# The next image's first layernorm: both halves abreast, with its additions ahead of the convolution's last taps

## The chip, the cores and the metric

The kernel runs on one core of a Trainium2 chip. The metric is device time in microseconds (us); a version's time is the median of its runs. Five engines matter: TensorE (PE; matmuls, weight loads are shown as PEld), VectorE (DVE), ScalarE (ACT), GpSimd (POOL; here it only issues DMAs that add into their destination, "folds") and SyncE (SP; plain DMAs). Each engine runs its own instructions in order and waits for semaphores that others raise.

## What is computed

Eight images of 384 channels and 32 x 32 positions go through a transformer block and then a ConvNeXt block, all in float32:

```python
# layer 0, per image: tokens xf of shape (1024, 384)
xn = layernorm(xf, g1, beta1)                    # "ln1", the first layernorm
q, k, v = xn @ w_qkv.T + b_qkv                   # 8 heads of 48
out = softmax(q @ k.T * SCALE) @ v
x1 = out @ w_proj.T + b_proj + xf
xn2 = layernorm(x1, g2, beta2)                   # "ln2", the second
h = gelu(xn2 @ w_fc1.T + b_fc1)                  # 384 -> 1536
x = x1 + h @ w_fc2.T + b_fc2
# layer 1, per image
y = depthwise_conv_7x7(x) + dw_b                 # 49 taps
y = layernorm(y, ln_w, ln_b)                     # "ln3", the third, over channels
y = gelu(y @ w1 + b1)
y = y * (gx / (mean(gx) + eps)) * gamma + beta + y   # gx: norm of each channel
x = x + y @ w2 + b2
```

## The kernel before

An image lies in SBUF as three tiles of 128 channels with 1024 positions each (`[P, CT, N]`); a "half" is 512 positions. Channels lie on partitions, so a layernorm over channels sums over partitions, with TensorE and a matrix of ones.

**One layernorm.** `layernorm` (from L486) makes a half in ten VectorE operations: two additions over the three channel tiles (L500, L503), three subtractions of the mean (L510), two additions of the three squares (L521, L524) and three scalings (L538). ScalarE makes the squares (L517) and the inverse root as a logarithm and an exponential (L534, L535). The sums over partitions are in `token_sums` (from L460). With `fold` it first lets GpSimd issue a DMA that adds one half of the partitions onto the other (L475), and then multiplies by 64 rows of ones instead of 128 (L481): half 0 uses partitions 0 to 63, half 1 uses 64 to 127. `abreast` runs the chains of both halves step by step together, `both` one after the other.

**The planner.** `Flow` writes the order of the instructions. Work beside the matmuls is a Python generator, a chain, that issues some instructions and yields a number of us of TensorE time after which it goes on. `flow.pe(us)` moves that clock by the planned length of a matmul (`U` = 0.857 us for a 128 x 512 one) and steps the chains that are due. `after(first, chain)` starts a chain when another has ended, `flow.finish` issues all that is left of one at once. So what stands ahead of what in an engine's queue is fixed when the program is built.

**One image.** For image b the order is: q and k, attention (with b + 1 loaded into `xn` in its middle), `mlp(b)`, then for image b - 1 `grn_up` (w1), the start of the convolution of b, values of b + 1 and `grn_down` (w2). `mlp` runs fc1 as 12 hidden tiles for half 0 and 12 for half 1 (`gelu_half`, L378: three matmuls of two passes each into a PSUM bank of the pool `ps_o`, four banks; a GELU by ScalarE, L457, empties it), while ln2 of half 1 runs beside them. Then `by_thirds` makes fc2 with 15 products of four matmuls each (L445) in place of 18, by sums and differences of the hidden tiles: pairs named e, f, g, h and d in the code, `hid` and `fc_e` in the profile. Most are made by VectorE in operations of 1024 columns (L953), g and the second h by folds (L965). Products of even number take a bank of `ps_o`, odd ones a tile of `ps_s` (two tiles of two banks). Results are added into `x` by VectorE (L950, L953) and copied into the padded image `pad` by ScalarE (L887).

**The convolution** of image b - 1 is 42 taps a channel tile on VectorE (L1098), spread over the stages before, and 7 that ScalarE multiplies and GpSimd's folds add (`help_convolution`, L1119, L1120; its scratch tiles have the tag `res`, four buffers). It must have ended before ln3 of image b - 1, and ln3 before `make_thirds` (L404, ten operations) and `grn_up` (L416).

**Where the two layernorms meet.** `conv_norm(b, ln)` is called in fc1 of image b, after hidden tile 3 of half 0, and starts two chains that wait for ln2's end: ln3 of image b - 1 (on `acc`, both halves abreast) and ln1 of image b + 1 (on `xn`). For b from 2 to 6, ln3's chain first issues the rest of the taps (`end_soon`), waits 16 us, and goes on with ln3's additions; ln1's chain waits 24 us and makes half 0 and then half 1 (`halves_of_next`). For b = 1, ln3 waits for the convolution's own end, and ln1 starts 1 us after ln2. Image 0 and image 7 go other ways.

Of the kernel before, what the change touches and what calls it, by code (L numbers as in the profile page):

```python
# [46 lines left out]
F32 = mybir.dt.float32  # L47
AF = mybir.ActivationFunctionType
ALU = mybir.AluOpType
AX = mybir.AxisListType  # L50

P = 128
B, C, H, W = 8, 384, 32, 32
N = H * W
CT = C // P
# [6 lines left out]
NH = N // 2  # L62
# [4 lines left out]
U = 0.857  # L67
# [108 lines left out]
def block_kernel(  # L176
# [15 lines left out]
    nc = tc.nc  # L192
# [5 lines left out]
    three = ctx.enter_context(tc.tile_pool(name="three", bufs=3))  # L198
# [3 lines left out]
    ps_s = ctx.enter_context(tc.tile_pool(name="ps_s", bufs=2, space=PSUM))  # L202
    ps_o = ctx.enter_context(tc.tile_pool(name="ps_o", bufs=4, space=PSUM))
    flow = Flow()
# [7 lines left out]
    def half(h):  # L212
        return slice(h * NH, (h + 1) * NH)
# [4 lines left out]
    def load_x(b, tag, parts=2, engine=nc.sync):  # L218
        xt = one.tile([P, CT, N], F32, tag=tag, bufs=2 if tag == "xn" else 1, name=f"{tag}_{b}")
        src = image_of(x, b).rearrange("(c p) n -> p c n", p=P)  # L220
        for i in range(parts):
            cols = slice(i * N // parts, (i + 1) * N // parts)
            engine.dma_start(out=xt[:, :, cols], in_=src[:, :, cols])
        return xt
# [4 lines left out]
    ones = const.tile([P, P], F32, name="ones")  # L229
    eps0 = const.tile([P, 1], F32, name="eps0")  # L230
# [19 lines left out]
    def col(name, i):  # L250
        at, width = VEC[name]
        assert i < width
        return vec[:, at + i : at + i + 1]
# [7 lines left out]
    def o_tile(name):  # L261
        return ps_o.tile([P, NH], F32, tag="o", name=name)
# [188 lines left out]
    def ln_table():  # L451
        if table[0] != "ln":
            nc.scalar.preload_act_table_set("natural_log_exp_and_others")
        table[0] = "ln"
# [5 lines left out]
    def token_sums(t, name, fold, wait):  # L460

        width = t.shape[-1]
        if fold is None:
            total = o_tile(name)[:, :width]
            nc.tensor.matmul(out=total, lhsT=ones, rhs=t, start=True, stop=True)  # L467
            flow.pe(U * width / NH)
            return [(total, slice(0, width))]
        rows = [slice(0, 64), slice(64, P)]  # L470
        parts = [(fold, slice(0, width))]
        if fold == "columns":
            parts = [(j, slice(j * width // 2, (j + 1) * width // 2)) for j in range(2)]
        for j, cols in parts:
            nc.gpsimd.dma_start(out=t[rows[j], cols], in_=t[rows[1 - j], cols], accum_op=ALU.add)  # L475
        yield wait
        totals = []
        for j, cols in parts:
            total = o_tile(f"{name}_{j}")[:, : cols.stop - cols.start]
            for i in rows:  # L480
                nc.tensor.matmul(out=total[i, :], lhsT=ones[rows[j], :64], rhs=t[rows[j], cols], start=True, stop=True)  # L481
            flow.pe(U * width / NH / 2)
            totals.append((total, cols))
        return totals

    def layernorm(src, dst, h, eps, g, name, switch, spare=None, spaced=False, slow=1.0, fold=None, wait=3.4, gentle=False):  # L486

        cols = h if isinstance(h, slice) else half(h)
        if isinstance(h, slice):
            h = h.start
        width = cols.stop - cols.start
        if spare:
            a, *squares = (t[:, :width] for t in spare())
            rstd = a
        else:
            a = one.tile([P, NH], F32, tag="ln_a", name=f"{name}_a{h}")[:, :width]
        nc.vector.tensor_tensor(a, src[:, 0, cols], src[:, 1, cols], ALU.add)  # L500
        if gentle:
            yield 1.2
        nc.vector.tensor_tensor(a, a, src[:, 2, cols], ALU.add)  # L503
        yield 2.6 * slow
        totals = yield from token_sums(a, f"{name}_sum{h}", fold, wait)
        yield 0.8
        for ct in range(CT):
            for total, part in totals:
                to, of = dst[:, ct, cols][:, part], src[:, ct, cols][:, part]
                nc.vector.scalar_tensor_tensor(to, total, -1.0 / C, of, ALU.mult, ALU.add)  # L510
            if gentle:
                yield 1.2
        yield 0.8 * slow
        if not spare:
            squares = [three.tile([P, NH], F32, tag="ln_sq", name=f"{name}_sq{h}_{ct}")[:, :width] for ct in range(CT)]
        for ct in range(CT):
            nc.scalar.activation(squares[ct], dst[:, ct, cols], AF.Square)  # L517
            if spaced:
                yield 1.7
        yield 0.8 if spaced else 1.8 * slow  # L520
        nc.vector.tensor_tensor(squares[0], squares[0], squares[1], ALU.add)  # L521
        if gentle:
            yield 1.2
        nc.vector.tensor_tensor(squares[0], squares[0], squares[2], ALU.add)  # L524
        yield 1.8 * slow
        totals = yield from token_sums(squares[0], f"{name}_var{h}", fold, wait)
        yield 0.8

        if not spare:
            rstd = one.tile([P, NH], F32, tag="ln_rstd", name=f"{name}_rstd{h}")[:, :width]  # L530
        if switch:
            ln_table()
        for var, part in totals:
            nc.scalar.activation(rstd[:, part], var, AF.Ln, bias=eps, scale=1.0 / C)  # L534
        nc.scalar.activation(rstd, rstd, AF.Exp, scale=-0.5)  # L535
        yield (2.6 if switch else 1.2) * slow
        for ct in range(CT):
            nc.vector.scalar_tensor_tensor(dst[:, ct, cols], dst[:, ct, cols], col(g, ct), rstd, ALU.mult, ALU.mult)  # L538
            if gentle and ct < CT - 1:
                yield 1.2  # L540
# [767 lines left out]
    def sequence(*chains):  # L1308
        for chain in chains:
            yield from chain  # L1310

    def after(first, chain, us=0):
        if us:
            yield us
        while first is not None and first.gi_frame is not None:
            yield 1.0
        yield from chain
# [293 lines left out]
    def main():  # L1611
# [5 lines left out]
        xn = load_x(0, "xn", 4)  # L1617
# [31 lines left out]
        t = three.tile([P, 2, NH], F32, tag="p", name="wqk_beta1").rearrange("p a n -> p (a n)")[:, : 2 * C]  # L1649
        for k in range(CT):  # L1650
            weighted(t, wqk_in(large[0])[:, k, :, :].rearrange("p m o -> p (m o)"), "beta1", k)
        ps = o_tile("bqk")
# [5 lines left out]
        state = {"help": None, "xn": xn, "conv": None, "acc": None, "norm1": None, "norm3": None}  # L1658
# [8 lines left out]
        def conv_norm(b, ln):  # L1667

            if b == 0:
                xn = state["xn"]  # L1670
                norm = abreast(xn, xn, eps0, "g1", "ln1_1", True, gentle=True)
                state["norm1"] = flow.spawn(after(ln, norm))
            else:
                acc = state["acc"]
                how = dict(wait=5.0) if b < B - 1 else dict(wait=3.4, factor=2.4)
                norm = abreast(acc, acc, eps1, "lnw", f"ln3_{b - 1}", True, **how)
                if 1 < b < B - 1:
                    state["norm3"] = flow.spawn(after(ln, sequence(end_soon(b), norm)))
                    state["norm1"] = flow.spawn(after(ln, halves_of_next(b, 24.0)))
                else:  # L1680
                    state["norm3"] = flow.spawn(after(ln, after(state["help"], after(state["conv"], norm))))
                if b == 1:
                    state["norm1"] = flow.spawn(after(ln, halves_of_next(b, 1.0)))

        def next_image(b):
            if b + 1 < B:
# [14 lines left out]

        def end_soon(b):
            end_convolution(b)
            yield 16.0

        def res_places(name):
            return [three.tile([P, NH], F32, tag="res", bufs=4, name=f"{name}_{i}") for i in range(4)]

        def halves_of_next(b, us):
            yield us  # L1710
            xn = state["xn"]
            for h in range(2):
                name = f"ln1_{b + 1}"
                places = lambda: res_places(f"{name}_{h}")
                yield from layernorm(xn, xn, h, eps0, "g1", name, True, spare=places, fold=h, wait=5.0, gentle=True)

        def before_fc2(b):

# [35 lines left out]
        for b in range(B):  # L1754
# [8 lines left out]
            ln2, rest, xn = attention(b, xt, *q_and_k, (folding, aside) if b == 0 else (), next_image)  # L1763
# [21 lines left out]
            if b < B - 1:  # L1785
# [4 lines left out]
                scale = flow.spawn(grn_scale(b - 1, gx, weights, b - 1, y))  # L1790
# [6 lines left out]
            else:  # L1797
# [4 lines left out]
                scale = flow.spawn(grn_scale(b - 1, gx, weights, b - 1))  # L1802
                flow.finish(state["norm_a"])
                sums = small.tile([P, CT, HT], F32, tag="gx_last", bufs=1, name="gx_last")
# [17 lines left out]
        scale = flow.spawn(grn_scale(B - 1, gx, weights, B - 1))  # L1822
# [143 lines left out]
```

## Time and profile before

| what | value |
|---|---|
| median of 3 runs | 3322.22 us (3320.67 to 3322.98) |
| the profiled execution, whole | 3318.74 us |
| its span, first to last instruction | 3316.9 us |
| granted TensorE clock, mean | 0.991 |
| L481, sums of 64 rows, ln1 (`ln_sum<-ln`) | 48 passes, median 640 ns |
| L1098, a tap on VectorE | 861, mean 1156 ns, 963.6 us busy |
| DMA into SBUF by GpSimd, `acc<-tap` | 294, 256 KB each, 3.6 us to landing |
| instructions | 38888 |

The span is one execution, taken by the hardware profiler. "Busy" counts overlapping instructions of an engine once. The profile names an instruction by engine, line and program names, with buffer numbers left out, so `ln<-ln` is any scratch tile of ln1. A matmul of float32 shows as two passes, so 'x4' there is two matmuls. A wait is put down to the semaphore that came last by the profile; where several came close together, it can have been another.

### The profile page before, as it was taken

What the parts mean: (1) busy time and instruction counts of PE and PEld (TensorE: products, weight loads), DVE (VectorE), ACT (ScalarE), POOL (GpSimd) and SP (SyncE); (2) the same over time, 40 slices, a digit from 0 to 9 for tenths busy, and PEclk for the clock granted to TensorE, in tenths of its full rate; (3) what the DMA queues carried; (4) which work ended last, traced back from release to release, by engine and by line L of the source; (5) the groups of instructions that cost most, each with busy time, mean ns of one, the idle gap of its engine ahead of it and who ended that gap; (6) DMA issues with size and microseconds to landing.
All of it is one profiled execution on the core that took longest, in us unless ns stands there. A gap on an engine that the chain in (4) does not pass through costs nothing. (4 is left out here: it accounts for less than half of the span.)

```text
span 3316.9 us, 38888 instructions
## 1 busy us (share of the span) xinstructions
PE 3260.0 (98%) x14216; PEld 1408.2 (42%) x14216; DVE 2431.7 (73%) x3318; ACT 1666.4 (50%) x2319; POOL 480.7 (14%) x567
## 2 busy tenths in 40 slices
PE   9999999999999999999999999999999999999999
PEld 5344434343344433444343443434434344444456
DVE  4644788787876878768787687866877778879850
ACT  3442763357644475354762647527474275723631
POOL 2121211112110121101211012110221102200000
PEclk9999999999999999999999999999999999999999
DMA  6635742547335573546635374353843538433231
GB/s 211 220 99 122 163 86 60 148 111 170 79 74 140 127 149 76 102 119 156 135 61 116 103 188 100 60 125 104 201 89 64 135 96 198 78 77 89 62 94 55
DMA packets 202707, 384.83 MB, mean 116 GB/s; under 512 B 41104, under 2 KB 47120, under 8 KB 202128
## 3 DMA queue, kind: packets, MB, share of 16 engines
q0 software_dynamic: 81472, 166.50, 26.8%
q1 hardware_dynamic: 120752, 215.09, 21.5%
q8 instruction: 114, 1.87, 0.2%
q10 hardware_dynamic: 288, 0.71, 0.1%
q14 instruction: 81, 0.66, 0.1%
HBM read 199.61 MB, written 38.14 MB: 72 GB/s over the span
## 5 line engine op out<-in xcount | busy, mean ns | idle before, releaser
L1098 DVE SCALAR_TENSOR_TENSOR acc<-pad,vec,acc 128x870 f32<-128x870 f32 (+8 forms) x861 | 963.6, 1156 | 6.6 <-DMA acc<-tap 1.7
L764 ACT ACTIVATE p<-s 128x1024 f32<-128x1024 f32 x512 | 524.6, 1025 | 275.3 <-PE s L755 267.3
L755 PE MATMUL s<-qk 48*64 48x512 f32 x4096 | 548.1, 593 | 0.2 <-ACT qk L601 0.2
L775 PE MATMUL o<-p,v 64*64 64x512 f32 x4096 | 545.6, 591 | 0.0
L378 PE MATMUL fc<-xn,fc 128*128 128x512 f32 x1152 | 505.0, 594 | 2.0 <-DVE acc L510 2.0
L1120 POOL DMA_DIRECT2D acc<-tap x294 | 253.6, 874 | 1337.6 <-ACT tap L1119 701.6
L378 PEld LDWEIGHTS fc<-xn,fc 128*128 128x128 f32 x1152 | 216.7, 190 | 286.0 <-issue 269.6
L445 PE MATMUL fc_p<-hid,fc 128*128 128x512 f32 x728 | 330.8, 611 | 0.0
L457 ACT ACTIVATE hid<-fc,bfc_f 128x512 f32<-128x512 f32 x192 | 131.1, 686 | 325.5 <-PE fc L378 325.4
L775 PEld LDWEIGHTS o<-p,v 64*64 64x64 f32 x4096 | 168.6, 133 | 275.8 <-issue 269.7
L755 PEld LDWEIGHTS s<-qk 48*64 48x64 f32 x4096 | 164.1, 133 | 276.4 <-issue 223.3
L445 PE MATMUL o_p<-y,w 128*128 128x512 f32 x624 | 270.9, 592 | 0.0
L445 PEld LDWEIGHTS fc_p<-hid,fc 128*128 128x128 f32 x728 | 141.5, 196 | 189.3 <-issue 185.4
L1119 ACT ACTIVATE tap<-pad,vec 128x512 f32<-128x512 f32 x294 | 215.9, 735 | 0.5 <-DMA acc<-tap 0.4
L445 PEld LDWEIGHTS o_p<-y,w 128*128 128x128 f32 x624 | 118.0, 190 | 148.7 <-issue 134.9
L1098 DVE SCALAR_TENSOR_TENSOR acc_last<-pad,vec,acc_last 128x377 f32<-128x377 f32 (+24 forms) x288 | 177.3, 690 | 0.6
L887 ACT COPY pad<-x 128x512 f32<-128x512 f32 x48 | 30.2, 634 | 285.6 <-DVE x L953 227.3
L716 DVE TENSOR_TENSOR attn<-o,attn 128x512 f32<-128x512 f32 x64 | 44.1, 689 | 124.5 <-ACT attn L714 124.5
L697 PE MATMUL proj<-attn,wproj_sb 128*128 128x512 f32 x288 | 127.7, 596 | 1.2 <-DVE attn L742 1.1
L675 PE MATMUL v<-wv_sb,xn 128*128 128x384 f32 x384 | 126.8, 487 | 0.0
L432 DVE TENSOR_TENSOR y<-h_n,y 128x512 f32<-128x512 f32 x72 | 49.8, 692 | 71.3 <-PE h_n L416 68.8
L675 PEld LDWEIGHTS v<-wv_sb,xn 128*128 128x128 f32 x384 | 72.5, 190 | 50.1 <-issue 3.3
(374 smaller groups left out, 4100.3 us busy)
## 6 DMA issues: line engine op xcount, KB each, us to landing
acc<-tap POOLq DMA_DIRECT2D x294, 256.0 KB, 3.6
fc<-s_fc SPq DMA_DIRECT2D x91, 256.0 KB, 4.3
w<-s_w SPq DMA_DIRECT2D x72, 320.0 KB, 3.0
hid<-hid POOLq DMA_DIRECT2D x42, 512.0 KB, 6.8
fc<-in_wfc SPq DMA_DIRECT2D x54, 384.0 KB, 4.0
w<-s_w SPq DMA_DIRECT2D x78, 256.0 KB, 2.7
y<-y POOLq DMA_DIRECT2D x36, 512.0 KB, 6.7
w_A<-in_w SPq DMA_DIRECT2D x36, 384.0 KB, 3.2
```

The lines of the kernel that those rows point to most:

```text
L378: nc.tensor.matmul(out=ps, lhsT=lhsT(k), rhs=rhs(k)[:, half(h)], start=(k == 0), stop=(k == nk - 1))
L432: nc.vector.tensor_tensor(c[dst], banks(name), c[other], ALU.add)
L445: nc.tensor.matmul(out=bank, lhsT=lhsT, rhs=rhs, start=k == 0, stop=k == len(pairs) - 1)
L457: nc.scalar.activation(dst, src, function, **kw)
L675: nc.tensor.matmul(out=ps[:, :C], lhsT=xn[:, k, t * P : (t + 1) * P], rhs=wv_sb[:, k, :], start=(k == 0), stop=(k == CT - 1),)
L697: nc.tensor.matmul(out=ps, lhsT=wproj_sb[:, m, ct * P : (ct + 1) * P], rhs=attn[:, m, :], start=(m == 0), stop=(m == CT - 1),)
L755: nc.tensor.matmul(out=s[64 * i : 64 * i + 64, j, :], lhsT=kT[64 * j : 64 * j + HD, m, k0 : k0 + 64], rhs=qT[64 * j : 64 * j + HD, m, half ...
L764: nc.scalar.activation(p, s, AF.Exp)
L775: nc.tensor.matmul(out=outs[i][64 * j : 64 * j + 64, :], lhsT=v[keys, t, at : at + 64], rhs=p[keys, j, :], start=(t == 0), stop=(t == KT - 1),
L1098: nc.vector.scalar_tensor_tensor(dst, window, tap, dst, ALU.mult, ALU.add)
L1119: nc.scalar.mul(t.rearrange("p (h w) -> p h w", w=W), window, tap)
L1120: nc.gpsimd.dma_start(out=acc[:, ct, half(h)], in_=t, accum_op=ALU.add)
```

## The change

`halves_of_next` is replaced by `norm_of_next`, which makes both halves of ln1 side by side:

- The four additions and the two folds of ln1 come as soon as ln2 has ended. Its chain is started before ln3's, so they stand ahead of the taps that `end_soon` issues.
- 22 us later (34 for b = 1) come the four sum matmuls, both halves one after the other, into tiles of `ps_s` instead of `ps_o`, then three subtractions a half, with squares of two channel tiles issued between them.
- The third square goes into the tile of the sums once the first addition of squares has read it, so that four `res` tiles serve both halves.
- After the folds of the squares it waits 8 us, then makes the variances, the inverse roots and six scalings, 1.2 us apart.
- For b = 1 the rest of the taps is also issued at ln2's end, with ln3's additions 28 us later.

```diff
@@ -1674,13 +1674,11 @@
                 acc = state["acc"]
                 how = dict(wait=5.0) if b < B - 1 else dict(wait=3.4, factor=2.4)
                 norm = abreast(acc, acc, eps1, "lnw", f"ln3_{b - 1}", True, **how)
-                if 1 < b < B - 1:
+                if b < B - 1:
+                    state["norm1"] = flow.spawn(after(ln, norm_of_next(b, 22.0 if b > 1 else 34.0)))
                     state["norm3"] = flow.spawn(after(ln, sequence(end_soon(b), norm)))
-                    state["norm1"] = flow.spawn(after(ln, halves_of_next(b, 24.0)))
                 else:
                     state["norm3"] = flow.spawn(after(ln, after(state["help"], after(state["conv"], norm))))
-                if b == 1:
-                    state["norm1"] = flow.spawn(after(ln, halves_of_next(b, 1.0)))
 
         def next_image(b):
             if b + 1 < B:
@@ -1701,18 +1699,63 @@
 
         def end_soon(b):
             end_convolution(b)
-            yield 16.0
-
-        def res_places(name):
-            return [three.tile([P, NH], F32, tag="res", bufs=4, name=f"{name}_{i}") for i in range(4)]
-
-        def halves_of_next(b, us):
+            yield 16.0 if b > 1 else 28.0
+
+        def norm_of_next(b, us):
+
+            xn, name = state["xn"], f"ln1_{b + 1}"
+            places = [three.tile([P, NH], F32, tag="res", bufs=4, name=f"{name}_{i}") for i in range(4)]
+            pairs = [(h, places[2 * h], places[2 * h + 1]) for h in range(2)]
+            rows = [slice(0, 64), slice(64, P)]
+
+            def fold(t, h):
+                nc.gpsimd.dma_start(out=t[rows[h], :], in_=t[rows[1 - h], :], accum_op=ALU.add)
+
+            def total(t, h, kind):
+                if kind == "sum":
+                    ps = ps_s.tile([P, N], F32, tag="s", name=f"{name}_sum{h}")[:, :NH]
+                else:
+                    ps = o_tile(f"{name}_var{h}")
+                for i in rows:
+                    nc.tensor.matmul(out=ps[i, :], lhsT=ones[rows[h], :64], rhs=t[rows[h], :], start=True, stop=True)
+                flow.pe(U / 2)
+                return ps
+
+            for h, a, _ in pairs:
+                nc.vector.tensor_tensor(a, xn[:, 0, half(h)], xn[:, 1, half(h)], ALU.add)
+            for h, a, _ in pairs:
+                nc.vector.tensor_tensor(a, a, xn[:, 2, half(h)], ALU.add)
+                fold(a, h)
             yield us
-            xn = state["xn"]
-            for h in range(2):
-                name = f"ln1_{b + 1}"
-                places = lambda: res_places(f"{name}_{h}")
-                yield from layernorm(xn, xn, h, eps0, "g1", name, True, spare=places, fold=h, wait=5.0, gentle=True)
+            sums = [total(a, h, "sum") for h, a, _ in pairs]
+            yield 0.8
+            for h, a, square in pairs:
+                for ct in range(CT):
+                    part = xn[:, ct, half(h)]
+                    nc.vector.scalar_tensor_tensor(part, sums[h], -1.0 / C, part, ALU.mult, ALU.add)
+                    if ct < 2:
+                        nc.scalar.activation((square, a)[ct], part, AF.Square)
+                yield 3.0
+            for h, a, square in pairs:
+                nc.vector.tensor_tensor(square, square, a, ALU.add)
+                nc.scalar.activation(a, xn[:, 2, half(h)], AF.Square)
+                yield 1.5
+            for h, a, square in pairs:
+                nc.vector.tensor_tensor(square, square, a, ALU.add)
+                fold(square, h)
+            yield 8.0
+            sums = [total(square, h, "var") for h, _, square in pairs]
+            yield 0.8
+            ln_table()
+            for h, a, _ in pairs:
+                nc.scalar.activation(a, sums[h], AF.Ln, bias=eps0, scale=1.0 / C)
+                nc.scalar.activation(a, a, AF.Exp, scale=-0.5)
+            yield 4.0
+            for h, a, _ in pairs:
+                for ct in range(CT):
+                    part = xn[:, ct, half(h)]
+                    nc.vector.scalar_tensor_tensor(part, part, col("g1", ct), a, ALU.mult, ALU.mult)
+                    yield 1.2
 
         def before_fc2(b):
```

## The prediction

> **What bounds the kernel now.** I read the page first, then the list of waits of TensorE, then the timeline of one image, then the granted clock after each stop.
>
> ```profile
> PE 3260.0 (98%) x14216; PEld 1408.2 (42%) x14216; DVE 2431.7 (73%) x3318; ACT 1666.4 (50%) x2319; POOL 480.7 (14%) x567
> ```
>
> TensorE is busy 3260.0 of 3316.9 us: only what shortens its work or its 57 us of idle time counts. (The chain of work that ended last reaches back only to 2946 us and shows the last image, which the change leaves alone.) The list of TensorE's waits over the span (total, times, longest, in us) puts half of the idle time on one place:
>
> ```profile
> PE ln_sum L481 <- DVE hid L953: 12.7, 3, 4.3
> PE ln_var L481 <- DMA ln<-ln: 8.9, 6, 3.5
> PE ln_sum L481 <- DMA ln<-ln: 7.9, 2, 4.0
> ```
>
> The tile `ln` is the scratch of the next image's first layernorm (ln1), so 12.7 + 8.9 + 7.9 = 29.5 us are waits of its sum matmuls. The timeline of image 2 (start, length, engine, line, operation, passes, idle time before it) shows where:
>
> ```profile
> 964.02 0.65 PE L481 MATMUL ln_sum<-ln_a,ones 64*64 64x512 f32 x2
> 965.04 6.28 PE L378 MATMUL fc<-xn,fc 128*128 128x512 f32 x14
> 965.14 3.68 DVE L510 SCALAR_TENSOR_TENSOR acc<-ln_sum,acc 128x512 f32<-128x512 f32 x6 [10.60 <-PE ln_sum L481]
> 971.25 1.08 PE L481 MATMUL ln_sum<-ln,ones 64*64 64x512 f32 x4
> 972.25 1.98 PE L378 MATMUL fc<-xn,fc 128*128 128x512 f32 x4
> ...
> 981.14 0.75 DVE L950 SCALAR_TENSOR_TENSOR x<-fc_p,vec,x 128x512 f32<-128x512 f32 x1 [6.62 <-PE fc_p L445]
> ...
> 1010.18 0.85 POOL L475 DMA_DIRECT2D ln<-ln  x1 [4.56 <-DVE ln L503]
> ...
> 1015.19 1.29 PE L481 MATMUL ln_sum<-ln,ones 64*64 64x512 f32 x4 [4.20 <-DVE hid L953]
> 1016.41 6.00 PE L445 MATMUL fc_p<-hid,fc 128*128 128x512 f32 x10
> ```
>
> Three things. The second half of ln1 is queued on VectorE among fc2's additions; its fold is issued only at 1010.18, and TensorE stands 4.20 us before the sum at 1015.19. (The releaser named is a VectorE addition that ended then. The fold that the sum needs takes 2.7 to 6.1 us to land there, so it comes down at the same moment; in two of the five images the fold itself is named.) VectorE meanwhile had 10.60 and 6.62 us idle, earlier. And the third layernorm (ln3), whose halves run abreast, needs 965.04 - 964.02 = 1.02 us of TensorE for both sums, ln1 972.25 - 971.25 = 1.00 us for one half. Last, 10 us windows from the restart after each long stop (length, TensorE busy, clock, DMA share and GB/s):
>
> ```profile
> 609.59:619.59 10.00, 10.00 (x17) 0.66 0.62 117
> 1015.19:1025.19 10.00, 10.00 (x21) 0.83 0.12 33
> 1418.02:1428.02 10.00, 10.00 (x21) 0.83 0.12 34
> 1819.54:1829.54 10.00, 10.00 (x19) 0.73 0.12 34
> 2221.69:2231.69 10.00, 10.00 (x18) 0.70 0.12 32
> 2624.25:2634.25 10.00, 10.00 (x18) 0.69 0.11 31
> ```
>
> The clock is below 1 after each: a "busy" TensorE is slow there.
>
> **What the Trainium skill says.** "TensorE: Matmul & The Clock Gate", Part 1 (The HAM clock gate): after an idle window of about 3.4 us TensorE falls to half clock until it has been busy for about as long. The trace agrees: idle of 3.46 to 4.28 us is followed by 0.66 to 0.83, idle of 1.08 us by none (a window from 1036.37 has 1.00). The same page, Part 3 (Packing small matmuls): matmuls on different row groups of the array run at the same time; the 1.02 against 1.00 us above is that. Its section "Architectural detail" calls ScalarE's and VectorE's queues strict FIFO; here a GELU (971.62) stands behind six squares. "DMA: Bandwidth & Descriptors", Anatomy of one DMA (SWDGE): about 2.0 us plus bytes by 436 GB/s, so an estimate of 2.3 us for a 131 KB fold. Here two folds that met little other traffic took 2.7 us, others up to 6.1.
>
> **The change part by part.** Image 2 (block b = 2) stands for b = 2 to 6, whose orders are alike; b = 1 is apart. Counts stay the same (20 VectorE operations, 10 ScalarE operations, 4 folds, 8 matmuls of 64 rows an image), SP's order too.
>
> *Gone: the idle time.* 3.46 us in b = 1, then 4.20 + 1.08, 4.28 + 1.07, 4.22 + 1.10, 3.87 + 1.08, 4.00 + 1.09: 29.5 us, if the new places of the sums have none.
>
> *Gone: the slow clock.* Ten us times one minus the clock: 3.4 + 1.7 + 1.7 + 2.7 + 3.0 + 3.1 = 15.6 us.
>
> *Gone: half of ln1's matmul time.* Sum and variance, one pair of 1.02 instead of two singles of 1.0: 2.0 us an image, 12.0 us. Together 57.1 us.
>
> *The additions ahead of the last taps.* Four additions at a pitch of 0.61 push the 13 taps back by 2.4 us: VectorE ends them at 952.9 instead of 950.4 and ln3's additions at 955.7 (953.2). ln3's folds then go out at about 954.4 and 956 and land, with the 5.6 and 6.2 us that the same two took, at 960 and 962. TensorE wants them at 964.2: covered by 2 us. In GpSimd's queue ln1's folds pass the first `fc2_e` fold, and nothing else waits there.
>
> *TensorE's new order* (0.43 us a pass). Hidden tile 6 of the second half starts at 956.3. After two of its matmuls come ln1's sums at 958.0; after two of tile 8 ln3's at 964.2; fc1 ends at 973.8; product 0 to 977.2; within product 1 ln1's variances at 978.9, after it ln3's at 981.7; product 2 at 982.7, 3 at 986.1, 4 at 989.6, 5 at 993.0.
>
> *The subtractions, squares and second additions.* ln1's six subtractions fill VectorE's idle time, 959.1 to 962.7. Before each ScalarE square stands one, so the GELU of tile 6 is at 961.0 instead of 958.98; its bank is wanted at 964.7. ln3's six: 965.3 to 968.9. Only then come ln1's additions (968.9, 969.5), so the third square of half 0 is at 969.6. Behind it on ScalarE stand six squares of ln3 (0.52 each), the third square of half 1 (973.3 to 973.9) and the GELUs of tiles 9 to 11, of which tile 9's is at 973.8 instead of 967.92. Their banks are wanted from 978.9, so no one waits. Half 1's last addition is over at 974.6, its fold lands 2.7 us after issue at 977.6, wanted at 978.9. ln3's four additions end at 977.6, the last fold lands at 980.6, wanted at 981.7. Both covers are only about 1.1 to 1.3 us.
>
> *The scalings: a new wait.* VectorE gets product 1 at 981.9, then two differences f (1.13 each), one scaling, two additions that wait for product 2 (986.3), a scaling, h0 (ends 989.4), ln3's six scalings (4.0), a scaling, h1 (ends 995.2), an addition for the thirds, x, a scaling, e0 (998.2), two more, e1 (1000.7). Before, one h and one e stood ahead of ln3's scalings: h1 ended at 988.8, e0 at 990.0 and e1 at 995.7. Product 5 wants h1 at 994.7 (0.5 late); product 6 wants e0 at 996.9 (1.3) and e1 at 1000.0 (0.75). New stalls: 2.55 us, too short for the clock to fall. The rest runs free: VectorE's next debts (f'' at 1017.7 for 1019.6, d at 1021.7 for 1026.5) are met, products 7 to 14 follow at 3.43 us. At the start of grn_up the copies for padding stand ahead of the first copy of `y`, some 0.2 us late, which the variance stop used to hide. Cost: 2.75 us an image, 13.8 us in five.
>
> *Block 1.* Its 21 taps are now emitted at once instead of spread, but end at about 559, and the sums stand after fc1's end (568.1), so these are covered. GpSimd's two g folds stand behind ln3's square folds, which end late. By the same rows: product 5 waits 0.9 for h1, ln3's variance 0.3, product 7 about 1.3 for its fold, products 11 and 12 0.8 and 1.6, and grn_up's fourth matmul 1.4 us more than the 1.88 it waits now for `y` behind late padding copies: 6.3. I take 5, since a later wait partly takes up an earlier one.
>
> *Sum.* 57.1 - 13.8 - 5 = 38.3 us. The profiled execution took 3318.7 us (span 3316.9 and 1.8 around it), so 3280.4; the median of the runs is 3.5 us above that execution, so 3322.2 - 38.3 = 3283.9 us.
>
> *Bounds.* The folds' landing has no row for its new traffic: with 2.3 us (the page's estimate) the stalls stay as above; with 6.1 (the longest here) each variance comes 2 to 3 us late, and ln3's scalings and h1, e0, e1 with it, 3 to 6 us an image. I take 2.7. VectorE's pitch is known, but a few operations in other places move h1 and e1 by 1.5 us either way, from no stall at all to 5 us an image. ScalarE's late GELUs cost 0 to 2.
>
> **The rivals.**
> *No new wait.* VectorE and the folds keep up everywhere: 57 us are won, 3265. For it: 17 us of idle VectorE in each image. Against: h1 and e0 stand behind six more scalings.
> *VectorE becomes the bound of fc2.* The differences come 5 to 6 us late in each image, the gain falls to about 57 - 30 - 7 = 20 us, 3302. For it: from 981 to 1002 VectorE has no idle time in my count. Against: ln1's whole second half has left it.
> *Slower: ScalarE's queue holds both layernorms.* The third square of ln1 stands ahead of ln3's squares and three GELUs, and itself behind ln3's subtractions. If ln3's folds land behind the sums, everything on ScalarE and the variances slip, and each stop of over 3.4 us costs the clock some 2.6 us more (15.6 by 6). An image breaks even when its new stops and slow clock reach 57.1 / 6 = 9.5 us: two stops of 3.5 with one clock loss. At 12 us an image the kernel takes 3322 + 15 = 3337. For it: covers of 1.1 to 2 us in a row. Against: the folds of before landed in time with the same neighbours.
> *It doesn't do what it says* is excluded: the order of instructions shows the pairs and the additions where described.
>
> **How the numbers follow.** Forecast (gain 25 to 50 us) 0.6; no new wait (50 to 58) 0.12; VectorE-bound (7 to 25) 0.16; no change 0.03; slower 0.09. Changes of 0.2% (6.6 us) are about what a measurement of this kernel can tell. Faster 0.88, same 0.03, slower 0.09. The range that leaves out 2 in 10 is a gain of 16 to 55 us: 3267 to 3306.
>
> **What would show it.** Right: the sum waits of ln1 are gone from TensorE's list; the windows at the old restarts have clock 1.00; waits of about 0.5 to 1.5 us of fc2's products on VectorE's `hid` and `fc_e` stand in each of b = 2 to 6; the 64-row sums take 1.0 us for both halves. Wrong: variances waiting for folds, GELU banks missing, or stops above 3.4 us in fc2.

## The result and the profile after

The changed kernel takes 3282.34 us (median of 4 runs, 3279.71 to 3285.09), the kernel before 3321.44 us beside it (4 runs, 3318.29 to 3322.98). The ratio is 0.9884, with a 95% interval of 0.9866 to 0.9901: 1.2% faster. Execution against execution, the two profiled ones took 3279.71 and 3318.74 us, a gain of 39.0; their spans are 3277.9 and 3316.9.

The busy line of the changed kernel's page, to be held against the one of before:

```profile
PE 3239.4 (99%) x14216; PEld 1399.7 (43%) x14216; DVE 2432.0 (74%) x3318; ACT 1662.0 (51%) x2317; POOL 480.3 (15%) x567
```

TensorE has the same 14216 passes in 20.6 us less, and its idle time fell by 18.4 us (from 56.9 to 38.5). VectorE's busy time is unchanged. So TensorE's work became faster, and fewer waits are left. Which waits, the list of TensorE's waits of the changed kernel shows (total, times, longest, in us):

```profile
PE fc_p L445 <- ACT fc_n L943: 5.6, 5, 1.1
PE h_n L416 <- ACT y L437: 2.5, 1, 2.5
PE fc_p L445 <- DVE hid L953: 2.4, 6, 0.6
PE fc_p L445 <- issue: 2.3, 1, 2.3
PE fc_p L445 <- DVE fc_e L953: 2.0, 5, 0.4
PE fc_p L445 <- DMA hid<-hid: 0.5, 1, 0.5
```

The three rows that held 29.5 us before, for the sums and variances of ln1, are gone. New are three waits in each of five images (5.6, most of 2.4, 2.0), and some in block 1. The longest wait of TensorE anywhere in the span is now 3.0 us, at the start of the run. The timeline of TensorE in image 2 (start, length, engine, line, operation, passes, idle time before it):

```profile
953.88 1.09 PE L1720 MATMUL ln_sum<-ln,ones 64*64 64x512 f32 x8
...
975.19 1.09 PE L1720 MATMUL ln_var<-ln,ones 64*64 64x512 f32 x8
976.21 1.98 PE L445 MATMUL fc_p<-hid,fc 128*128 128x512 f32 x4
...
982.68 8.75 PE L445 MATMUL fc_p<-hid,fc 128*128 128x512 f32 x20
991.80 1.98 PE L445 MATMUL fc_p<-hid,fc 128*128 128x512 f32 x4 [0.37 <-DVE hid L953]
994.90 1.96 PE L445 MATMUL fc_p<-fc_e,fc 128*128 128x512 f32 x4 [1.12 <-ACT fc_n L943]
997.25 1.98 PE L445 MATMUL fc_p<-fc_e,fc 128*128 128x512 f32 x4 [0.40 <-DVE fc_e L953]
```

Eight passes of 64 rows, both halves of ln1, take 976.21 - 975.19 = 1.02 us. (A product is eight passes.) The second half of product 5 waits 0.37 us, the two halves of product 6 wait 1.12 and 0.40. What they wait for stands on VectorE:

```profile
987.87 2.07 DVE L538 SCALAR_TENSOR_TENSOR acc<-acc,vec,attn 128x512 f32<-128x512 f32 x3
989.86 0.74 DVE L1757 SCALAR_TENSOR_TENSOR xn<-xn,vec,ln 128x512 f32<-128x512 f32 x1
990.52 1.22 DVE L953 TENSOR_TENSOR hid<-fc_e,hid 128x1024 f32<-128x1024 f32 x1
...
992.92 0.74 DVE L1757 SCALAR_TENSOR_TENSOR xn<-xn,vec,ln 128x512 f32<-128x512 f32 x1
993.58 1.22 DVE L953 TENSOR_TENSOR fc_e<-hid 128x1024 f32<-128x1024 f32 x1
...
995.98 1.22 DVE L953 TENSOR_TENSOR fc_e<-hid 128x1024 f32<-128x1024 f32 x1
```

The difference h1 ends at 991.74, and the second half of product 5 starts at 991.80. The difference e0 ends at 993.58 + 1.22 = 994.80, and the first half of product 6 starts at 994.90. The releaser named there is a ScalarE copy that ended at 994.40; TensorE did not start then, so it waited for e0. The scalings of ln1 (L1757) stand between the differences.

### The profile page after: what moved, and what is told of

Its sections match the earlier page's. It is cut to its first block, busy times and chain, and to the rows that moved or that the text cites. A ratio compares the mean times of both kernels' runs of the same rounds, so it can differ in the third digit from the quotient of the medians.

```text
span 3277.9 us, 38879 instructions
## 1 busy us (share of the span) xinstructions
PE 3239.4 (99%) x14216; PEld 1399.7 (43%) x14216; DVE 2432.0 (74%) x3318; ACT 1662.0 (51%) x2317; POOL 480.3 (15%) x567
## 5 line engine op out<-in xcount | busy, mean ns | idle before, releaser
L445 PE MATMUL fc_p<-hid,fc 128*128 128x512 f32 x728 | 319.7, 594 | 5.2 <-DVE hid L953 2.4
```

Of the source, the lines that this page charges most:

```text
L445: nc.tensor.matmul(out=bank, lhsT=lhsT, rhs=rhs, start=k == 0, stop=k == len(pairs) - 1)
```

## The experiments

The first four ran together, beside a kernel before of 3318.51 us; the last three together, beside 3318.58 us. Times are medians; each ratio is to the kernel before that ran beside it. The changed kernel itself ran on another occasion, beside 3321.44 us, so a difference to its median holds to a few us only, and the timelines decide what an edit did.

**One row group instead of two.** Both halves of ln1 are folded onto partitions 0 to 63, so that all four matmuls of a sum use the same row group of TensorE's array. The order stays the same.

```diff
-                nc.gpsimd.dma_start(out=t[rows[h], :], in_=t[rows[1 - h], :], accum_op=ALU.add)
+                nc.gpsimd.dma_start(out=t[rows[0], :], in_=t[rows[1], :], accum_op=ALU.add)
...
-                    nc.tensor.matmul(out=ps[i, :], lhsT=ones[rows[h], :64], rhs=t[rows[h], :], start=True, stop=True)
+                    nc.tensor.matmul(out=ps[i, :], lhsT=ones[rows[0], :64], rhs=t[rows[0], :], start=True, stop=True)
```

> The changed kernel, but both halves of ln1 are folded onto partitions 0 to 63, so that all four matmuls of a sum use one row group of TensorE. Theory (a pair on two row groups runs at the price of one, the 12.0 us term): a pair of halves takes 2.0 us instead of 1.02, twice an image, six images: 12 us more than the changed kernel, about 3294 us, ratio to the kernel before 0.992. Rival (the pairs save nothing, the gain is idle time and clock alone): as the changed kernel, 3282 us, and the eight passes still take about 1.0 us.

Measured: 3290.1 us, ratio 0.9918 (0.9901 to 0.9934), 7.8 us above the changed kernel's median (11 us by the two ratios). TensorE's timeline of this run:

```profile
976.61 1.94 PE L1720 MATMUL ln_var<-ln,ones 64*64 64x512 f32 x8
978.47 1.98 PE L445 MATMUL fc_p<-hid,fc 128*128 128x512 f32 x4
```

The same eight passes take 978.47 - 976.61 = 1.86 us instead of 1.02. Measured at grn_up's first matmul, images 2 to 6 lose 1.69 to 1.83 us each, about 1.7, which is twice 0.84. In block 1 the loss is made up again by a wait for `y` of 0.80 us instead of 2.50. So the two halves do run at once in the changed kernel, and by this count that is worth some 10 us over six images. The 12 us expected took a pair on one row group to need 2.0 us.

**ln1's scalings later.** The changed kernel, with the six scalings 30 us after the inverse roots instead of 4 us, for b from 2 to 6.

```diff
-            yield 4.0
+            yield 30.0 if b > 1 else 4.0
             for h, a, _ in pairs:
```

> The changed kernel, with ln1's six scalings 30 us after the inverse roots instead of 4 us for b = 2 to 6. Theory (products 5 and 6 wait because these scalings stand ahead of the differences h1, e0 and e1): the three waits of 0.37, 1.12 and 0.40 us an image go, and none comes in products 12 and 14, where the differences had 1.9 us and more to spare: 9.5 us less than the changed kernel, about 3273 us, ratio 0.9855. Rival (ln3's six scalings alone make them late, or a bank that ScalarE empties, as the profile names it): the waits stay within 0.5 us of what they are, 3282 us.

Measured: 3270.12 us, ratio 0.9852 (0.9836 to 0.9868). TensorE's timeline over the same products:

```profile
984.52 10.46 PE L445 MATMUL fc_p<-hid,fc 128*128 128x512 f32 x24
994.82 3.60 PE L445 MATMUL fc_p<-fc_e,fc 128*128 128x512 f32 x8
998.26 4.03 PE L445 MATMUL fc_p<-hid,fc 128*128 128x512 f32 x9
```

The three waits are gone and no other takes their place. From the start of product 3 to that of product 7 the time is 998.26 - 984.52 = 13.74 us, against 999.08 - 982.68 = 16.40 in the changed kernel: 2.66 us. Images 2 to 6 are each shorter by 2.16 to 2.66 us. The named waits of image 2 add up to only 1.89. The rest, 0.77, I call the drain: four passes started 0.43 us apart take 1.72 us of the matmul flow but are listed with 1.98, so each wait begins to count about 0.26 us after the next matmul could have started.

**The clock, without the idle time.** This is the kernel before, with five matmuls on constant data (into the bank of the sum, which overwrites them) in the stop ahead of half 1's sum, or variance for b = 1. They fill the stop and compute nothing. The line numbers from there on are two higher.

(The lines that set `warm` to 5 at these places are left out.)

```diff
             total = o_tile(f"{name}_{j}")[:, : cols.stop - cols.start]
+            for _ in range(warm):
+                nc.tensor.matmul(out=total[:, :C], lhsT=ones, rhs=wproj_sb[:, 0, :], start=True, stop=True)
             for i in rows:
```

> The kernel before, with five matmuls of 128x384 of constants (3.2 us of work with no reader) put into the long stop of each image, ahead of half 1's sum of ln1 (its variance for b = 1). They add work that nothing waits for; the stop ends when it did. Theory (after a stop of over 3.4 us TensorE runs at half clock for some us, the 15.6 us term): the clock in the 10 us after each stop is 1.00 instead of 0.66 to 0.83, and the kernel takes 12 to 15 us less than before, about 3307 us, ratio 0.9958. Rival (the slow passes wait for weights or operands): no faster than before, 3321 us or some us more.

Measured: 3306.95 us, ratio 0.9968 (0.9953 to 0.9982). TensorE's timeline at the stop of image 2, then the ten us after all six stops (length, TensorE busy, clock, DMA share and GB/s):

```profile
1009.35 3.39 PE L481 MATMUL ln_sum<-wproj_sb,ones 128*128 128x384 f32 x10
1013.75 1.08 PE L483 MATMUL ln_sum<-ln,ones 64*64 64x512 f32 x4 [1.01 <-DVE hid L955]
1014.76 5.42 PE L445 MATMUL fc_p<-hid,fc 128*128 128x512 f32 x12
```
```profile
611.48:621.48 10.00, 10.00 (x25) 1.00 0.73 150
1013.75:1023.75 10.00, 10.00 (x25) 1.00 0.19 51
1413.39:1423.39 10.00, 9.99 (x25) 1.00 0.19 50
1813.78:1823.78 10.00, 10.00 (x25) 1.00 0.20 54
2214.78:2224.78 10.00, 10.00 (x25) 1.00 0.19 53
2615.20:2625.20 10.00, 10.00 (x25) 1.00 0.19 53
```

The sum still comes when its fold allows it, but the clock is 1.00 at all six places, where it was 0.66 to 0.83. From the start of fc1 to grn_up's first matmul, the six blocks are shorter by 3.39, 1.61, 3.17, 2.08, 2.61 and 2.71 us: 15.6 in all (about 0.6 of the third is a chance wait of the kernel before at 1324.5). So the clock costs 15 us of its own, apart from the idle time. The total moved by 11.6 only: the rest of the program, which is the same, took 3.8 us more in this execution, 2.2 of them ahead of the first fc1.

**The additions behind the taps.** The changed kernel with its two chains started in the other order, so that the rest of the taps stands ahead of ln1's additions again.

```diff
-                    state["norm1"] = flow.spawn(after(ln, norm_of_next(b, 22.0 if b > 1 else 34.0)))
                     state["norm3"] = flow.spawn(after(ln, sequence(end_soon(b), norm)))
+                    state["norm1"] = flow.spawn(after(ln, norm_of_next(b, 22.0 if b > 1 else 34.0)))
```

> The changed kernel with the two chains started in the other order, so that ln1's additions stand behind the last taps and ahead of ln3's additions. By the rows of the changed kernel the additions then end at about 948.8 us in image 2 and the folds land at 951 to 953, where the sums want them at 953.9. Theory (the gain comes from side by side and early sums; the place ahead of the taps is only cover): as the changed kernel within 3 us, 3282 us, ratio 0.988. Rival (the additions must stand ahead of the taps): the sums wait 2 us or more an image for their folds, 10 us or more in all, 3292 us or above.

Measured: 3281.15 us, ratio 0.9888 (0.9871 to 0.9904), no different from the changed kernel. VectorE makes the additions at 947.60 to 950.0 instead of 931 to 933.5, and TensorE's sums come at 955.27 without a wait. That part of the change is cover and brings nothing measurable by itself.

**Side by side, but begun late.** The changed kernel with all of ln1 moved back: for b from 2 to 6 its chain waits 24 us, as before, and its sums come 8 us after the additions.

```diff
+            if b > 1:
+                yield 24.0
+                us = 8.0
             for h, a, _ in pairs:
                 nc.vector.tensor_tensor(a, xn[:, 0, half(h)], xn[:, 1, half(h)], ALU.add)
```

> The changed kernel, both halves of ln1 still side by side, but for b from 2 to 6 begun where the kernel before began (24 us after ln2, behind the taps and ln3's additions; sums 8 us after that). Theory (what took ln1's second half out of fc2's additions is that the halves run side by side; the early start is cover): the sums of ln1 now stand about 9 us later, behind ln3's, the variances about 10 us later, inside product 4. No wait of 3.5 us, the clock stays near 1, pairs still take 1.02 us. Some 4.6 us of VectorE work (three subtractions, four additions) slip into fc2 ahead of the differences, so stalls of 0 to 4 us an image replace the 1.9 of the changed kernel: 3282 to 3296, about 3287, ratio 0.9895. Rival (the early start is what matters): the folds are late again, stops of 3 us or more and a slow clock return in each image, 5 x 6 us: 3310 or more, ratio 0.997 or above.

Measured: 3267.72 us, ratio 0.984 (0.9825 to 0.9855). Both theories missed: the rival by over 40 us, mine by 14 us at the other end. TensorE and, below it, VectorE in image 2 of this run (line numbers from L1725 on are three higher):

```profile
980.95 0.65 PE L481 MATMUL ln_var<-ln_sq,ones 64*64 64x512 f32 x2
...
990.75 1.09 PE L1720 MATMUL ln_var<-ln,ones 64*64 64x512 f32 x8
991.77 4.56 PE L445 MATMUL fc_p<-hid,fc 128*128 128x512 f32 x10
996.16 3.60 PE L445 MATMUL fc_p<-fc_e,fc 128*128 128x512 f32 x8
```
```profile
986.67 1.22 DVE L953 TENSOR_TENSOR hid<-fc_e,hid 128x1024 f32<-128x1024 f32 x1
...
991.78 1.22 DVE L953 TENSOR_TENSOR fc_e<-hid 128x1024 f32<-128x1024 f32 x1
...
994.18 1.21 DVE L953 TENSOR_TENSOR fc_e<-hid 128x1024 f32<-128x1024 f32 x1
...
997.84 1.41 DVE L1760 SCALAR_TENSOR_TENSOR xn<-xn,vec,ln 128x512 f32<-128x512 f32 x2
```

ln1's variances now stand behind ln3's, and without a wait. My count charged VectorE for the work that slips into fc2, but not the work that slips out at the other end: the first scaling of ln1 (L1760) is at 997.84, behind h1, e0 and e1 (e1 ends at 995.39; product 6 starts at 996.16). Images 2 to 6 each gain 2.65 or 2.66 us over the changed kernel, just what the stalls cost. So the early start isn't needed, and by bringing the scalings early it is what causes the stalls. Halves side by side are enough; no run made them one after the other but early, so what an early start alone would bring is not shown.

**The scalings later in block 1 too.**

```diff
-            yield 4.0
+            yield 30.0
             for h, a, _ in pairs:
```

> The changed kernel with ln1's six scalings 30 us after the inverse roots in every block, b = 1 too (the run e2_scalings_later had this for b from 2 to 6). Theory: in block 1 VectorE is without idle time from 601 us to the end of fc2 there, and the six scalings (4.0 us) stand ahead of f'' and of the last additions into x. Four of them now come after those, two just ahead: the waits for f'' (0.6 us) and for y behind the late padding copies (2.5 us) shrink to together about 1; nothing else changes. About 1 to 2 us below e2_scalings_later: 3268.5, ratio 0.9847. Rival (the waits of block 1 come from the folds and TensorE's own products, not from VectorE): same as e2_scalings_later, 3270, or 1 us above.

Measured: 3266.54 us, ratio 0.9841 (0.9827 to 0.9854), the lowest median of the study, though its interval overlaps those of the two runs at 3267.72 and 3270.12. Against the other run with late scalings, block 1 is 3.96 us shorter up to grn_up and gives back 0.62 by its attention, but not all of that is the edit. In that run the fold that the second half of product 7 needs cost 1.96 us, and the ten us behind it had clock 0.83; in the changed kernel, whose block 1 has the same instructions, it cost 0.50. Against the changed kernel block 1 is 2.51 us shorter up to grn_up: the wait of 2.25 us ahead of product 12, for f'', is gone, with its drain. The wait for `y` did not shrink as I expected, but grew to 3.12 us: TensorE comes earlier, and two scalings stand just ahead of the last additions into `x`, behind which the padding copies and then `y` wait.

**ln1's sums in `ps_o`.**

```diff
-                if kind == "sum":
-                    ps = ps_s.tile([P, N], F32, tag="s", name=f"{name}_sum{h}")[:, :NH]
-                else:
-                    ps = o_tile(f"{name}_var{h}")
+                ps = o_tile(f"{name}_{kind}{h}")
```

> The changed kernel with ln1's two sums in banks of ps_o instead of tiles of ps_s. Theory: each bank of the two is free again when VectorE has made the subtractions, 2 and 4 us after the sums; the tile that comes four banks later starts some 5 to 8 us after them, so no hidden tile waits more than 0.5 us: 3282 to 3285, ratio 0.989, no long stop. Rival (ps_s is part of the gain, since ln1's and ln3's sums and the hidden tiles share four banks and ScalarE's GELUs are late there): fc1's matmuls wait for GELUs by 1 to 3 us in each image, 3288 to 3300.

Measured: 3282.64 us, ratio 0.9888 (0.9873 to 0.9903), the same as the changed kernel. No hidden tile waits for a bank in image 2; the pool makes no difference here.

## Why the prediction was right, point by point

The forecast was a gain of 38.3 us, 3284 us for the median. The medians give 39.1, execution against execution 39.0. The mechanism came out as foretold in images 2 to 6, and for the most part in block 1. That the sum is right to 1 us is partly luck: it leaves out some 2.9 us of drain that were won, and on the other side a slow stretch of 1.5 us in block 1 and 0.9 us that images 2 to 6 gave back; and parts that no edit touched move by more than 1 us between executions.

- *Idle time of the sums, 29.5.* All of it is gone; none of ln1's sums or variances waits in blocks 1 to 6. With the drain of some 0.26 us at each of 11 stops the true loss was nearer 32.
- *Slow clock, 15.6.* Right: 15 in the run with filled stops. In images 2 to 6 of the changed kernel no slow stretch is left. In block 1 a new one comes. Ten us windows at the stop of block 1 in the kernel before, at the new place of image 2's variances, and after the wait for `y` in block 1 show

```profile
609.59:619.59 10.00, 7.75 (x19) 1.00 0.57 156
975.19:985.19 10.00, 10.00 (x35) 1.00 0.31 83
632.81:642.81 10.00, 10.00 (x20) 0.85 0.78 288
```

  The first has 2.25 us of the wait for f'' in it: TensorE is idle there, and the clock holds. The third follows a stop of 2.50 us and loses 1.5 us. The prediction held stops under 3.4 us to be too short for that and put nothing for it.
- *Pairing, 12.0.* Of this some 10 us are the two row groups (1.7 an image). The remaining 2 us may come from having the halves in one place instead of two, which no run took apart.
- *Order and covers.* With image 2 shifted by 4.13 us, the time won by fc1's start, the sums foretold for 958.0 and 964.2 came at 958.0 and 964.4, the variances foretold for 978.9 and 981.7 at 979.3 and 982.3. The folds of the squares landed in 2.7 to 3.7 us from issue (the trace's DMA list for 966 to 978 us: a median of 2.8 for the two of ln1, 2.7 and 3.7 for those of ln3), against 2.7 taken, and kept 1.3 and 0.8 us of the cover. From the figures of the Trainium skill ("DMA: Bandwidth & Descriptors", Anatomy of one DMA) the prediction's estimate for such a fold was 2.3 us; no fold of ln1 landed in less than 2.7 here.
- *Stalls of the scalings.* I had 2.55 us an image: h1 0.5, e0 1.3, e1 0.75. The places are right and the named waits are smaller (0.37, 1.12, 0.40), but with the drain the loss is 2.66, shown by the run with later scalings. That the stalls come from the scalings, and not from VectorE as a whole, is shown by the same run: with as many operations on VectorE they vanish.
- *Block 1, 5 us.* Its waits are 0.57 at product 5, 0.50 at the g fold, 2.25 ahead of product 12 (the list says "issue"; VectorE's operation that makes f'' ends at 617.09, the product starts at 617.19) and 2.50 for `y`, 0.62 more than before. That makes 3.9 us, to which the drains and the 1.5 us of slow clock come; the waits foretold for product 7 and grn_up's share came smaller, the one for f'' larger. Up to image 2 the block gained 3.2 us, where 3.46 + 3.4 + 2.0 - 5 = 3.9 was foretold.
- *Images 2 to 6* won 6.69 to 7.86 us each up to grn_up, 36.8 in all, and gave back 0.1 to 0.5 each before the next attention: 35.9, where 34.4 (38.3 less 3.9) was foretold.

The rivals: *VectorE becomes the bound of fc2* had the right place, but differences that come 5 to 6 us late; in images 2 to 6 they held TensorE up by 1.12 us at most at one place, and cost 2.66 us in image 2. *Slower, by ScalarE's queue* did not happen: the third square of half 1 was done at 969.94, the GELU of tile 9 followed it, and nothing waited for either. *No new wait*, at 3265, describes not this kernel but its neighbours with the scalings moved: 3266.5 to 3270.

The best version of the study is the changed kernel with its scalings 30 us after the inverse roots in every block, 3266.54 us, or equally the side-by-side layernorm begun late, 3267.72. What is left open is why block 1 alone keeps a wait of 2.5 to 3 us for `y`, of which this study only shows that the last additions into `x` lead to it.

## What to carry to other kernels

When a stop of TensorE is removed, look for three parts of its cost: the named wait, the drain ahead of it, and a slow clock behind it, which the busy share hides. Then ask which work of the moved chain nobody needs soon, here the last six scalings, and place it behind the work that others wait for; moving a chain early brings its unurgent tail early too. A new place for a step is counted on both sides, with what slips in and what slips out; counting one side alone missed by 14 us here.

## What the runs showed of the hardware

- Each of the six stops of 3.5 to 4.3 us was followed by half clock. It lasted 3.4 or 6.8 us. In image 2 of the kernel before all of it lay behind the restart at 1015.19, in image 4 a part lay ahead of the restart at 1819.54:

```profile
1015.93:1019.34 3.41, 3.41 (x6) 0.50 0.00 0
1818.06:1824.89 6.83, 5.35 (x8) 0.50 0.07 25
```

  So stops of nearly the same length cost 1.6 to 3.4 us more in clock. Stops cut to about 1 us cost none.
- The Trainium skill ("TensorE: Matmul & The Clock Gate", Part 1) puts the edge at an idle window of about 3.4 us, and the prediction said that the trace agrees. Below that edge it does not: shorter stops went either way. The stop ahead of product 12 in block 1 lasted 2.25 us in the run with one row group and 2.48 us in the run with the sums in `ps_o`; the ten us behind it were, in this order,

```profile
619.26:629.26 10.00, 10.00 (x20) 0.83 0.16 40
622.26:632.26 10.00, 10.00 (x24) 1.00 0.23 66
```

  In the kernel before a stop of 1.93 us near 172 us was followed by 0.83, one of 1.88 us at 638 us by 1.00.
- The four matmuls of 64 rows that sum both halves take 1.02 us on two row groups and 1.86 on one. The same page's Part 3 (Packing small matmuls) says that matmuls on different row groups run at the same time; the first experiment shows it by a change of the row group alone.
- Between executions, parts of the program that no edit touched moved by several us: the start of the first fc1 lay between 208.0 and 212.9 us, the wait for the first bias `b` near 120 us was 3.0 to 6.0 us long, the fold of an early layernorm near 172 us waited for 1.9 to 3.1. Differences of 1 to 5 us between kernels are better read stage by stage than from the total.
